# Layer-0 attention loop: keys in two halves instead of three batches, and each engine's work of a step in longer runs

## The chip, the cores and the metric

The kernel runs on one core of a Trainium2 chip, as one launch. The metric is the device time of that core in microseconds. Three runs of the kernel before took 2561.23, 2567.15 and 2571.44 us, the median is 2567.15 us. One more execution was taken with the hardware profiler; all readings below come from it. Its engines are called PE (TensorE matmul), PEld (TensorE weight load), DVE (VectorE), ACT (ScalarE), POOL (GpSimd) and SP (SyncE, here the issuer of most DMAs).

## What is computed

Four residual layers with layer normalisation work on the same 2708 x 2708 adjacency matrix and 2708 x 512 features, all in float32. The change lies in layer 0, a masked attention with 8 heads of 64 dimensions:

```python
keys = jnp.einsum('nj,hjk->hnk', node_matrix, Wks)
queries = jnp.einsum('nj,hjk->hnk', node_matrix, Wqs)
values = jnp.einsum('nj,hjk->hnk', node_matrix, Wvs)
atts = jnp.einsum('hqk,hmk->hqm', queries, keys) / key_dim ** 0.5
atts = atts - 1e+16 * (1.0 - adj)[None, :, :]
atts = jax.nn.softmax(atts, axis=-1)
return jnp.einsum('hqm,hmk,hko->qo', atts, values, Wo)
```

Layers 1 to 3 (two graph convolutions and a graph attention with one score vector) follow; the change does not edit their code.

## The kernel before

First, keys, queries and values are projected (to about 208 us of the profile). Then comes the loop of layer 0 (208 to 1237 us), the output product with `Wo`, and the three other layers.

**Items and steps.** The 2708 nodes are 22 chunks of 128 rows (`NC`; the last, `LAST`, has 20). An item of the loop is one chunk of query rows and one pair of heads: 21 x 4 items and one item for the short last chunk with all heads together, 85 in all. In step i the loop works on four items at once: `new` (item i, its scores), `cur` (item i-1, its softmax weights and their transposition), `late` and `old` (items i-2 and i-3, their value sums).

**Scores (L402, L424).** For one item the 2708 keys are cut into three batches of 1024, 1024 and 660 (`ends`), each into two parts. For each part PE makes one product per head into a PSUM bank (64 x 512 or 64 x 330; float32, so every product shows as two matmul instructions). DVE reads the bank, adds the mask row, writes the scores to SBUF and keeps the maximum: 12 such instructions per item. L439 reduces the maxima.

**Weights (L446).** ACT takes the exponentials in place, one per batch and head: six per item.

**Transposition.** The value sums need the weights with keys on partitions. For 16 of the 22 key chunks (0 to 15, "dealt") DVE transposes 32 x 32 blocks into a tile `d` (L453, four instructions of 128 x 1024 per item), and four DMAs issued by SP (L463, `deal`, 256 KB each) carry the tile from partition to partition into a tile `e`. An item has two deals, one per batch of 8 chunks. The remaining six chunks are transposed by PE (L482, L489, L491, `turn`) into PSUM and copied to SBUF by ACT.

**Value sums (L509).** 22 key chunks x 2 heads, two instructions each, 88 per item, accumulate into one PSUM bank; ACT copies it out (L529) and POOL stores it.

**Order.** PE, DVE and ACT run the loop in the order in which it is written (`tc.manual_schedule`); a planner orders the other queues, SP's and POOL's, by its own costs. On PE a step is: two parts of scores, 8 chunks of value sums of `old`, two parts of scores, 14 chunks of value sums of `late`, two parts of scores, 12 transposes of `cur`. On DVE: four score instructions, the block transposes of the first batch, four score instructions, the block transposes of the second batch, four score instructions, the maxima. So the first deal of `cur` starts in the middle of a step and is used by `late` about one step later, and the second starts near the step's end and is used by `old` in the step after the next.

**Buffers.** PSUM has 8 banks: 2 x 2 for scores (`ps_s`), 3 for PE transposes (`ps_t`), 1 for value sums (`ps_a`). In SBUF there are five score tiles, two tiles `d` and three tiles `e`; a block transpose that reuses a tile `d` waits until the deal that read it has landed. Of the mask for the next chunk, one third is loaded (L169), summed (L187), given its diagonal (L201) and scaled (L207) in each of three of the four steps of a chunk.

Of the kernel before, what the change touches and what calls it, by code (L numbers as in the profile page):

```python
# [10 lines left out]
ALU = mybir.AluOpType  # L11
# [11 lines left out]
def kernel(  # L23
# [65 lines left out]
    def rsqrt(dst, v, q, n, tag):  # L89

        y0 = small.tile([P, n], F32, tag=f"{tag}y0", name=f"{tag}_y0")
        t = small.tile([P, n], F32, tag=f"{tag}t", name=f"{tag}_t")
        nc.scalar.activation(t[:q], v, AF.Ln)  # L93
        nc.scalar.activation(y0[:q], t[:q], AF.Exp, scale=-0.5)
        t2 = small.tile([P, n], F32, tag=f"{tag}t2", name=f"{tag}_t2")
        nc.vector.tensor_tensor(t2[:q], y0[:q], y0[:q], ALU.mult)
        t3 = small.tile([P, n], F32, tag=f"{tag}t3", name=f"{tag}_t3")
        nc.vector.scalar_tensor_tensor(t3[:q], t2[:q], -0.5, v, ALU.mult, ALU.mult)
        nc.vector.scalar_tensor_tensor(dst, t3[:q], 1.5, y0[:q], ALU.add, ALU.mult)
# [18 lines left out]
    ND = ends[2]  # L118
    KD4 = P // 32
    SW = max(min(b * P, N) - a * P for a, b in zip(ends, ends[1:]))  # L120
# [6 lines left out]
    smt = [const.tile([P, HALF0, 2 * NP, NW], F32, tag=f"smt{i}", name=f"smt{i}") for i in range(2)]  # L127
# [10 lines left out]
    with ExitStack() as l0:  # L138
# [70 lines left out]
        with tc.tile_pool(name="kvw", bufs=1) as kvw, tc.tile_pool(name="xTb", bufs=2) as xtp, tc.tile_pool(  # L209
# [64 lines left out]
            for b in order:  # L274
# [15 lines left out]
                for c in chunks_of(b):  # L290
# [3 lines left out]
                    if c < ND:  # L294
# [79 lines left out]
        ps_t = l0.enter_context(tc.tile_pool(name="ps_t", bufs=3, space=PSUM, reuse_waits="tile"))  # L374
        ps_a = l0.enter_context(tc.tile_pool(name="ps_a", bufs=1, space=PSUM, reuse_waits="tile"))
        ps_s = l0.enter_context(tc.tile_pool(name="ps_s", bufs=2, space=PSUM, reuse_waits="tile"))
        sp = l0.enter_context(tc.tile_pool(name="sp", bufs=5, reuse_waits="tile"))
        dp = l0.enter_context(tc.tile_pool(name="dp", bufs=2, reuse_waits="tile"))
        ep = l0.enter_context(tc.tile_pool(name="ep", bufs=3, reuse_waits="tile"))
        ptp = l0.enter_context(tc.tile_pool(name="ptp", bufs=1, reuse_waits="tile"))  # L380

        class Pair:


            def __init__(self, c, p):
                self.c, self.p = c, p
                self.s = []
                self.mx = [
                    small.tile([P, 2 * NW], F32, tag=f"mx{j}", name=f"mx{c}_{p}_{j}") for j in range(2)
                ]  # L390
# [20 lines left out]
            def scores(self, k, part):  # L411
# [3 lines left out]
                n0, w = batch(k)  # L415
                if part == 0:
                    self.s.append(sp.tile([P, 2, SW], F32, tag="s", name=f"s{c}_{p}_{k}"))
                s = self.s[k]
                h0 = part * (w // 2)
                hw = w - w // 2 if part else w // 2  # L420
                pss = [ps_s.tile([P, BLK], F32, tag=f"s{j}", name=f"pss{c}_{p}_{k}_{part}_{j}") for j in range(2)]
                self.products(pss, n0 + h0, hw)
                for j in range(2):
                    nc.vector.tensor_tensor_reduce(  # L424
                        out=s[:, j, h0 : h0 + hw],
                        in0=pss[j][:, :hw],
                        in1=a[:, n0 + h0 : n0 + h0 + hw],
# [4 lines left out]
                        accum_out=self.mx[j][:, 2 * k + part : 2 * k + part + 1],  # L432
                    )

            def maxima(self):
                c, p = self.c, self.p
                self.nm = [small.tile([P, 1], F32, tag=f"nm{j}", name=f"nm{c}_{p}_{j}") for j in range(2)]
                for j in range(2):
                    nc.vector.tensor_reduce(self.nm[j], self.mx[j], AX.X, ALU.max, negate=True)  # L439

            def weights(self, k):

                w = batch(k)[1]
                for j in range(2):
                    s = self.s[k][:, j, :w]
                    nc.scalar.activation(s, s, AF.Exp, bias=self.nm[j], accum_out=self.sums(j, k))  # L446

            def blocks(self, k, j):

                n = ends[k + 1] - ends[k]  # L450
                if k not in self.D:
                    self.D[k] = dp.tile([P, KD4, 2, n, 32], F32, tag="d", name=f"d{self.c}_{self.p}_{k}")
                nc.vector.transpose(  # L453
                    self.D[k][:, :, j].rearrange("p i m x -> p m i x"),
                    self.s[k][:, j, : n * P].rearrange("p (m i x) -> p m i x", i=KD4, x=32),
                )

            def deal(self, k):

                n = ends[k + 1] - ends[k]  # L460
                e = ep.tile([P, KD4, 2, n, 32], F32, tag="e", name=f"e{self.c}_{self.p}_{k}")
# [5 lines left out]
                self.E[ends[k]] = e  # L467

            def turn(self):

                c, p = self.c, self.p
                last = NC - 2
                o, mr = (NC - 1 - ND) * P, rows(NC - 1)[1]

                def part(j, m):
                    return self.s[2][:, j, (m - ND) * P : (m - ND) * P + P]

                for j in range(2):
                    pt = ps_t.tile([P, last - ND, P], F32, tag="t", name=f"pst{c}_{p}_{j}")
                    sb = ptp.tile([P, last - ND, P], F32, tag="pt", name=f"pt{c}_{p}_{j}", bufs=2)  # L480
                    for m in range(ND, last):
                        nc.tensor.transpose(pt[:, m - ND, :], part(j, m), ident)  # L482
                    nc.scalar.copy(sb, pt)  # L483
                    for m in range(ND, last):
                        self.pts[m, j] = sb[:, m - ND, :]
                pt = ps_t.tile([P, 4, P], F32, tag="t", name=f"pst{c}_{p}_2")
                sb = ptp.tile([P, 2, P], F32, tag="pt2", name=f"pt{c}_{p}_2")
                for j in range(2):
                    nc.tensor.transpose(pt[:, j, :], part(j, last), ident)  # L489
# [911 lines left out]
```

## Time and profile before

| | us |
|---|---|
| runs, median (lowest to highest) | 2567.15 (2561.23 to 2571.44) |
| span of the profiled execution, first to last instruction | 2565.8 (its own device time is not listed apart; the median stands 1.35 above the span) |
| stages of the span: projections / loop of layer 0 / the rest | 0 to 208 / 208 to 1237 / 1237 to 2566 |
| busy in 270 to 740, of 470.0: PE, DVE, ACT | 469.2, 456.7, 378.1 |
| the same stretch: granted TensorE clock, DMA share, DMA rate | 1.00, 0.84, 220 GB/s |
| first and last instruction of L439 (two per step): start | 216.5 and 1209.6 |

A group of the profile has the line of the kernel, the engine, what is written and read, the shape and the count, then busy time and the mean of one instruction. The chain is followed back from the last instruction to what released each; in order of time its pieces have start, length, engine, tile and line. In the table of stretches, each engine has its busy time and in brackets its number of instructions, followed by the granted clock, the share of time that the 16 DMA engines were busy, and the rate.

### The profile page before, as it was taken

To read this page: it belongs to the slowest core of one execution; us is meant where nothing else is said; L and a number is where in the kernel's file an instruction comes from. 1 tells how busy PE (TensorE), PEld (TensorE's weight loads), DVE (VectorE), ACT (ScalarE), POOL (GpSimd) and SP (SyncE) were. 2 spreads that over 40 slices of the span, in tenths; PEclk is the share of its full clock that TensorE was granted. 3 is DMA by queue.
4 is the path that set the end of the run, shared out by engine and by line. 5 is a ranking of instruction groups with operands and counts; after the bars stand their busy time and mean duration, and the time that the engine had idled before them with its cause. 6 is when DMAs were issued, how large, how long until landed. Compare 5 with 4: busy or idle time off the path is not lost.

```text
span 2565.8 us, 42805 instructions
## 1 busy us (share of the span) xinstructions
PE 2511.8 (98%) x15551; PEld 1523.6 (59%) x15551; DVE 1958.5 (76%) x4711; ACT 1208.1 (47%) x2410; POOL 315.9 (12%) x322
## 2 busy tenths in 40 slices
PE   9999999999999999999999999899999999999997
PEld 4886766667676767666555445444444466444465
DVE  2669999999999999999474778987876874443544
ACT  2105788787887887887011002565665540000000
POOL 1210000000000000000310000343433430000000
PEclk9999999999999999999899999999999999999999
DMA  5115888888888888888753444444433214644633
GB/s 176 45 58 135 228 217 213 231 212 231 221 208 233 212 213 235 215 215 197 223 174 106 124 118 142 133 155 125 140 109 110 57 30 115 191 139 143 177 99 109
DMA packets 221502, 411.46 MB, mean 160 GB/s; under 512 B 28765, under 2 KB 48911, under 8 KB 221292
## 3 DMA queue, kind: packets, MB, share of 16 engines
q1 hardware_dynamic: 215052, 392.00, 56.0%
q0 software_dynamic: 6240, 16.73, 1.7%
q8 instruction: 123, 2.02, 0.3%
q14 instruction: 87, 0.71, 0.1%
HBM read 213.55 MB, written 16.72 MB: 90 GB/s over the span
## 4 chain that ended last, share of the span: by engine, by line
PE 78%; issue 9%; DVE 7%; DMA 3%; ACT 1%; SPq 1%; POOL 0%; POOLq 0%; DVEq 0%; ACTq 0%
PE pss L402 15%; PE av L509 15%; PE acc L823 12%; PE acc L929 7%; PE m L1233 6%; PE pst L482 3%; PE pf L835 3%; PE po L769 2%; PE psk L253 2%; PE psv L253 2%; PE psq L253 2%; DMA e<-d 2%; PE ph L915 1%; DVE d L453 1%; DVE s L424 1%
## 5 line engine op out<-in xcount | busy, mean ns | idle before, releaser
L424 DVE CUSTOM_DVE_ANT_0 s<-pss,adj 128x512 f32<-128x512 f32 (+1 forms) x1020 | 574.3, 618 | 23.2 <-PE pss L402 21.3
L446 ACT ACTIVATE s<-s,nm 128x1024 f32<-128x1024 f32 (+1 forms) x510 | 527.7, 1037 | 26.6 <-DVE nm L439 25.0
L402 PE MATMUL pss<-KT,qt 64*128 64x512 f32 (+1 forms) x2016 | 460.2, 565 | 4.2 <-DVE mx L424 4.2
L453 DVE STREAM_TRANSPOSE d<-s 128x1024 f32<-128x1024 f32 x340 | 402.4, 1222 | 9.7 <-ACT s L446 4.8
L823 PE MATMUL acc<-pt,x 128*128 128x512 f32 (+1 forms) x880 | 334.7, 539 | 12.0 <-ACT pt L876 9.7
L509 PEld LDWEIGHTS av<-e,V 128*64 128x64 f32 x5376 | 294.6, 137 | 62.7 <-DMA e<-d 41.7
L509 PE MATMUL av<-e,V 128*64 128x128 f32 x5376 | 326.3, 274 | 0.0
L402 PEld LDWEIGHTS pss<-KT,qt 64*128 64x128 f32 x2016 | 191.8, 186 | 140.5 <-issue 67.7
L823 PEld LDWEIGHTS acc<-pt,x 128*128 128x128 f32 x880 | 158.7, 193 | 187.7 <-issue 162.7
L929 PE MATMUL acc<-at,h 128*128 128x512 f32 (+1 forms) x504 | 196.8, 543 | 0.0
L887 POOL TENSOR_TENSOR cs<-cs,pt 128x512 f32<-128x512 f32 (+2 forms) x110 | 157.3, 1430 | 202.9 <-ACT pt L876 199.8
L874 DVE TENSOR_TENSOR pt<-pt,at 128x512 f32<-128x512 f32 (+2 forms) x132 | 107.3, 820 | 74.6 <-ACT pt L873 74.2
L530 POOL DMA_DIRECT2D otd<-ot x84 | 45.2, 538 | 965.4 <-ACT ot L529 953.0
L1263 ACT ACTIVATE z<-pz,rdeg 128x512 f32<-128x512 f32 (+1 forms) x22 | 15.1, 688 | 311.1 <-PE pz L835 311.1
L93 ACT ACTIVATE ln_t<-lnve 128x1 f32<-128x1 f32 x88 | 17.7, 201 | 301.5 <-DVE lnve L107 301.3
L929 PEld LDWEIGHTS acc<-at,h 128*128 128x128 f32 x504 | 90.2, 190 | 101.4 <-issue 99.0
L483 ACT COPY pt<-pst 128x512 f32<-128x512 f32 x170 | 91.4, 589 | 120.4 <-PE pst L482 120.3
L509 PEld LDWEIGHTS av<-pt,V 128*64 128x64 f32 x1680 | 90.0, 136 | 64.6 <-ACT adj L187 46.2
L876 ACT ACTIVATE pt<-pt 128x512 f32<-128x512 f32 (+2 forms) x132 | 76.1, 578 | 108.8 <-DVE pt L875 108.7
L940 DVE SCALAR_TENSOR_TENSOR cs<-at,rdeg,cs 128x512 f32<-128x512 f32 (+2 forms) x126 | 86.2, 684 | 40.8 <-DMA at<-in_adjT_dram 39.7
L509 PE MATMUL av<-pt,V 128*64 128x128 f32 x1680 | 110.3, 278 | 1.4 <-ACT ot L529 1.4
L482 PEld LDWEIGHTS pst<-ident,s 128*128 128x128 f32 x680 | 73.5, 141 | 38.8 <-issue 38.3
(352 smaller groups left out, 3627.6 us busy)
## 6 DMA issues: line engine op xcount, KB each, us to landing
e<-d SPq DMA_DIRECT2D x680, 256.0 KB
at<-in_adjT_dram SPq DMA_DIRECT2D x210, 256.0 KB
a<-in_adj_dram SPq DMA_DIRECT2D x38, 677.0 KB
adj<-in_adj_dram SPq DMA_DIRECT2D x42, 512.0 KB
at_a<-in_adjT_dram SPq DMA_DIRECT2D x40, 256.0 KB
at_c<-in_adjT_dram SPq DMA_DIRECT2D x40, 256.0 KB
at_f<-in_adjT_dram SPq DMA_DIRECT2D x40, 256.0 KB
adj<-in_adj_dram SPq DMA_DIRECT2D x21, 330.0 KB
```

Of the source, the lines that this page charges most:

```text
L253: nc.tensor.matmul(ps[:, p, :], ws[i][:, k, p * P : (p + 1) * P], xs[i][:, k, :], start=(k == 0), stop=(k == FC - 1),)
L402: nc.tensor.matmul(pss[j][:, :w], qt[h, self.p, :], KT[h, self.p, n0 : n0 + w], start=True, stop=True)
L424: nc.vector.tensor_tensor_reduce(out=s[:, j, h0 : h0 + hw], in0=pss[j][:, :hw], in1=a[:, n0 + h0 : n0 + h0 + hw], scale=1.0, scalar=LOW, o ...
L446: nc.scalar.activation(s, s, AF.Exp, bias=self.nm[j], accum_out=self.sums(j, k))
L453: nc.vector.transpose(self.D[k][:, :, j].rearrange("p i m x -> p m i x"), self.s[k][:, j, : n * P].rearrange("p (m i x) -> p m i x", i=KD4 ...
L482: nc.tensor.transpose(pt[:, m - ND, :], part(j, m), ident)
L509: nc.tensor.matmul(self.av[j * KD : (j + 1) * KD, out], V[:, m, h * KD : (h + 1) * KD], weights[j], start=(self.done == 0), stop=(self.don ...
L823: nc.tensor.matmul(acc[k][:, :w], last[0][g : g + mr, :] if m == NC - 1 else values[:mr, k * P : (k + 1) * P], moving[g : g + mr, :w], sta ...
L874: nc.vector.tensor_tensor(pt[:mr, :w], pt[:mr, :w], at[:mr, :w], ALU.subtract)
L887: nc.gpsimd.tensor_tensor(sums[:mr, :w], sums[:mr, :w], pt[:mr, :w], ALU.add)
L929: nc.tensor.matmul(acc[hc][:, :w], lastH[g : g + mr, :] if m == NC - 1 else H[m][:mr, hc * P : (hc + 1) * P], at[g : g + mr, :w], start=(m ...
L1233: nc.tensor.matmul(acc[k][:, : moving.shape[1]], combined[which, m][:, k * P : (k + 1) * P], moving, start=(m == 0), stop=(stop and m == N ...
```

## The change

The keys are cut into two halves, 1408 and 1300 (`bounds`), each into three parts of 469, 469, 470 and 433, 433, 434 keys. In each half the first 8 chunks are dealt (0 to 7 and 11 to 18); PE transposes the other six (8, 9, 10, 19, 20, 21). The exponentials are four per item, the block transposes two per item (each for both heads, 2048 columns), the maxima one instruction. Scores and PE transposes share 7 PSUM banks in rotation; the bank of the value sums stays. Score tiles are two per half; tiles `d` and `e` stay two and three.

The written order of a step is now: on PE all scores of `new`, all value sums of `late` (the PE-transposed chunks first, then the two deals), all transposes of `cur`; on DVE all 12 score instructions, the maxima, the two block transposes of `cur`, each followed by its deal; on ACT the exponentials of `cur`'s second half, the work on the next mask, the exponentials of `new`'s first half, the copy of the value sums, the copies of the transposes. `old` is gone, and the loop has one step less at its end. In `rsqrt`, scratch tiles that are wider than one column get one buffer instead of four.

```diff
     NW = 3
     ends = [0, 8, 16, NC]
-    ND = ends[2]
+    HALVES = 2
+    PARTS = 3
+    DEALT = 8
+    bounds = [0, NC // 2, NC]
+    def dealt(c):
+        return any(a <= c < a + DEALT for a in bounds[:-1])
+    turned = [c for c in range(NC) if not dealt(c)]
...
-                    if c < ND:
+                    if dealt(c):
...
-        ps_t = l0.enter_context(tc.tile_pool(name="ps_t", bufs=3, space=PSUM, reuse_waits="tile"))
         ps_a = l0.enter_context(tc.tile_pool(name="ps_a", bufs=1, space=PSUM, reuse_waits="tile"))
-        ps_s = l0.enter_context(tc.tile_pool(name="ps_s", bufs=2, space=PSUM, reuse_waits="tile"))
-        sp = l0.enter_context(tc.tile_pool(name="sp", bufs=5, reuse_waits="tile"))
+        ps_s = l0.enter_context(tc.tile_pool(name="ps_s", bufs=7, space=PSUM, reuse_waits="tile"))
+        sp = l0.enter_context(tc.tile_pool(name="sp", bufs=2, reuse_waits="tile"))
         dp = l0.enter_context(tc.tile_pool(name="dp", bufs=2, reuse_waits="tile"))
         ep = l0.enter_context(tc.tile_pool(name="ep", bufs=3, reuse_waits="tile"))
...
+        ready = turned + [c for c in range(NC) if dealt(c)]
...
-                h0 = part * (w // 2)
-                hw = w - w // 2 if part else w // 2
+                h0, h1 = (w * i // PARTS for i in (part, part + 1))
...
-            def blocks(self, k, j):
+            def blocks(self, k):
+                self.D[k] = dp.tile([P, KD4, 2, DEALT, 32], F32, tag="d", name=f"d{self.c}_{self.p}_{k}")
                 nc.vector.transpose(
-                    self.D[k][:, :, j].rearrange("p i m x -> p m i x"),
-                    self.s[k][:, j, : n * P].rearrange("p (m i x) -> p m i x", i=KD4, x=32),
+                    self.D[k].rearrange("p i j m x -> p j m i x"),
+                    self.s[k][:, :, : DEALT * P].rearrange("p j (m i x) -> p j m i x", i=KD4, x=32),
                 )
...
-            def values(self, m0, m1):
+            def values(self):
...
-                for m in range(m0, m1):
+                for m in ready:
...
-            for i in range(len(items) + 3):
+            for i in range(len(items) + 2):
                 if cur is not None:
-                    cur.weights(0)
+                    cur.weights(1)
                 if i < len(items):
...
-                    new.scores(0, 0)
-                    new.scores(0, 1)
-                if old is not None:
-                    old.values(ends[1], ND)
-                if prep:
-                    row_sums(c + 1, p - 1)
-                if cur is not None:
-                    cur.weights(1)
-                    cur.blocks(0, 0)
-                    cur.blocks(0, 1)
-                    cur.deal(0)
...
-                    new.scores(1, 0)
-                    new.scores(1, 1)
-                if cur is not None:
-                    cur.weights(2)
-                if late is not None:
-                    late.values(ND, NC)
-                    late.values(0, ends[1])
-                if cur is not None:
-                    cur.blocks(1, 0)
-                    cur.blocks(1, 1)
-                    cur.deal(1)
...
+                    for part in range(PARTS):
+                        new.scores(0, part)
+                    if prep:
+                        row_sums(c + 1, p - 1)
+                    new.scores(1, 0)
+                    if prep:
+                        loops(c + 1, p - 1)
+                        mask(c + 1, p - 1)
+                    for part in range(1, PARTS):
+                        new.scores(1, part)
                     new.maxima()
+                    new.weights(0)
...
+                if late is not None:
+                    late.values()
                 if cur is not None:
+                    for k in range(HALVES):
+                        cur.blocks(k)
+                        cur.deal(k)
                     cur.turn()
...
-                old, late, cur = late, cur, new
+                late, cur = cur, new
```

## The prediction

> **What bounds the kernel now.** I read the chain first. On the page it is mostly PE:
>
> ```profile
> PE 78%; issue 9%; DVE 7%; DMA 3%; ACT 1%; SPq 1%; POOL 0%; POOLq 0%; DVEq 0%; ACTq 0%
> ```
>
> The same chain in order of time, inside the loop, is PE alone. One step:
>
> ```profile
> 310.93 1.92 PE pss L402 x8
> 312.85 1.90 PE av L509 x32
> 314.74 1.92 PE pss L402 x8
> 316.66 3.21 PE av L509 x56
> 319.87 1.31 PE pss L402 x8
> 321.18 1.02 PE pst L482 x8
> 322.20 0.22 PE pst L489 x2
> 322.42 0.22 PE pst L491 x2
> ```
>
> The pieces add to 11.72 us: PE never waits here. Over the loop the 84 intervals between the maxima (L439, 216.5 to 1209.6 us) average 11.82 us; the 0.1 more is steps in which mask loads get in the way. Next the timeline of DVE, to see how close the second engine is:
>
> ```profile
> 706.55 0.69 DVE L424 CUSTOM_DVE_ANT_0 s<-pss,adj 128x512 f32<-128x512 f32 x1
> ...
> 710.88 0.50 DVE L424 CUSTOM_DVE_ANT_0 s<-pss,adj 128x330 f32<-128x330 f32 x1
> ...
> 711.30 0.50 DVE L424 CUSTOM_DVE_ANT_0 s<-pss,adj 128x330 f32<-128x330 f32 x1
> ...
> 714.59 2.37 DVE L453 STREAM_TRANSPOSE d<-s 128x1024 f32<-128x1024 f32 x2
> ```
>
> Starts are 0.61 us apart at 512 columns (from 706.55 to 707.16) and 0.42 at 330. A step has 8 x 0.61 + 4 x 0.42 + 2 x 2.33 for transposes + 0.37 for maxima and hand-over = 11.6 us of 11.72. DVE is 0.1 us from being the bound. Third, DMA, over one step whose block transposes end at 705.24 and 710.14:
>
> ```profile
> 705.24:707.24 2.00, 2.00 (x42) 2.00 (x40) 2.00 (x8) 2.00 (x5) 0.00 (x0) 1.00 0.39 59
> 707.24:712.24 5.00, 5.00 (x46) 3.54 (x44) 4.87 (x17) 4.14 (x10) 0.00 (x0) 1.00 0.90 210
> 712.24:717.24 5.00, 5.00 (x53) 2.91 (x51) 5.00 (x11) 4.34 (x10) 0.54 (x1) 1.00 0.80 210
> ```
>
> A deal is slow to start (59 GB/s for 2 us) and then runs at 210 GB/s with the DMA engines 80 to 90% busy: 256 KB (262,144 bytes) in 1.25 us. The trace's completion records give the landings: deal one all landed 7.28 us after its block transposes ended, deal two 7.83 us after its own, at 717.97. Nobody waits: `late` reads the first at 718.0 (landed 712.5), `old` reads the second at 724.65. What a deal does with something ahead of it in the queue shows near the loop's end:
>
> ```profile
> 1160.57 0.60 SPq L463
> 1161.22 1.10 SPq L463
> 1162.66 5.49 DMA e<-d
> 1168.37 2.37 DVE d L453 x2
> ```
>
> Its transposes had ended at 1158.06; it landed at 1168.15, 10.1 us later, and DVE stood waiting for tile `d`.
>
> **The change part by part.** Lengths are from the profiled execution, and the sum is made on its span of 2565.8 us.
>
> *PE gains.* 24 value-sum instructions more take 3.21 - 1.90 = 1.31 us: 54.6 ns each, so a run costs 0.15 us to enter (1.90 - 32 x 0.0546). A score run of 8 costs 1.92 us at 512 columns and 1.31 at 330: 3.35 ns a column, 0.20 to enter. Going from three score runs to one and from two value runs to one saves 2 x 0.20 + 0.15 = 0.55 us: 11.72 becomes 11.17 us. Twelve banks through a rotation of seven cost nothing: the hiding work is DVE's 0.55 us per bank against PE's 0.40; if PE had no lead left, its run would stretch to DVE's pace, up to 1.6 us, still beside DVE's work.
>
> *DVE gains little.* The columns are the same. From 0.61 and 0.42, (0.61 - 0.42)/182 = 1.04 ns a column; 469 columns cost 0.565 us, 433 cost 0.527; six of each 6.55. One reduction instead of two, with hand-over, 0.25; two transposes of 2048 columns 2.3 each (two of 1024 took 2.37). Sum 11.4 us, call it V. Without new waits the step would be the larger of 11.17 and 11.4.
>
> *ACT.* Exponentials of 1024 take 1.14 us and of 660 take 0.83, so 1408 take 1.47 and 1300 take 1.38: 5.7 us instead of 6.2. With mask work (1.25 + 1.14) and copies (2.2) it has 10.3 us of work in the fullest steps. New order: the copies that free PSUM banks queue behind `new`'s first exponentials, which wait for the maxima. At 11.4 us a step this leaves about 1 us of slack; beyond that scores would wait for banks.
>
> *The deals lose their lead: the cost.* Both deals now start at the end of DVE's step, 2.3 us apart instead of 5 to 7, and `late` reads both in the very next step. Call L the time from the end of the second block transposes to the landing of the second deal. It is not seen directly. From below: a deal by itself, 7.6 us. From above: 10.1 us as at 1158, plus what mask loads in front add (deals behind three mask loads landed after 8.64 and 9.72 us instead of 7.28 and 7.83), about 12. Between: eight DMAs back to back take 2 + 8 x 1.25 = 12.0 us from the end of the first block transposes by the rate; by the landings in the step above 12.7 us (705.24 to 717.97, no pause in between). Less the 2.3 us, L is 9.7 to 10.4. I take 10.2, nearest to the landings.
>
> From that landing the path runs on PE: the last 32 value instructions 1.75, twelve transposes 1.46, entries 0.3, then the next scores until DVE can begin, 1.1 (PE started at 722.73 and DVE at 723.89 with 512 columns): 4.6 us. PE works in order, so the next scores cannot pass the waiting value sums. Then comes DVE's whole step V to the end of its second block transposes. A deal issued at the end of step n holds back the scores of step n+2, so two steps take 2T = L + 4.6 + V = 10.2 + 4.6 + 11.4 = 26.2, T = 13.1 us. This is above both engines' own times, so it sets the pace. A second wait lies just under it: the second block transposes reuse tile `d`, which the deal of the step before still reads, T >= L + 2.3 = 12.5.
>
> *SP.* It still issues eight deal DMAs a step, and the third and fourth of a deal were held 1.0 to 1.5 us each at issue; now eight stand in one row, and the mask loads (1.6 MB per four steps) queue among them. Before they cost the mean 0.1 us a step; I keep that: T = 13.2 us.
>
> *The end of the loop.* Before, the load of `wo` was issued at 1221.5, 12 us after the last maxima, right behind the last deal. Now both deals of the last item follow two block transposes that wait for tile `d`: between -3 (one step less) and +9 us; I take +4. Everything with one answer: dealing chunks 11 to 18 instead of 8 to 15 changes addresses of as many POOL copies, the scratch buffers of `rsqrt` are used one step at a time, the dropped `old` adds no work: 0.
>
> Sum: (13.2 - 11.82) x 84 = +116, +4 at the end: 2565.8 + 120 + 1.35 (median over span) = 2687 us, +4.7%.
>
> **Two rules weighed.** The Trainium skill, "DMA: Bandwidth & Descriptors", section on the anatomy of one DMA (it describes the gpsimd path), gives about 2.0 us plus bytes at 436 GB/s. As an estimate by that page, both deals would be through 2.0 + 4.8 = 6.8 us after the first block transposes, L = 4.5, and the step would be DVE's 11.4. The rows above moved the same bytes at half that rate, so the measurement decides.
> "TensorE: Matmul & The Clock Gate", section on HAM oscillation, warns that idle gaps over about 3.4 us halve PE's clock. The rows show clock 1.00 in 270 to 740 us, where PE idled 0.8 of 470 us, so no row tests it inside the loop. If each pair of steps tripped one such window, the page would add, as an estimate, 42 x 1.7 = 71 us.
>
> **The rivals.**
> - *No new wait.* If a second deal needed L <= 2 x 11.4 - 4.6 - 11.4 = 6.8 us and tile `d` came free in time, T = 11.4: 2567 - 0.42 x 84 = 2532 us. For it: PE and DVE both have less to do. Against: even a deal alone took 7.3 to 7.8.
> - *The gain and the wait cancel.* L = 7.6, as if the first deal did not delay the second: T = 11.8, 2567 us. Against: 80 to 90% busy DMA engines with two deals half as close.
> - *Deals stream faster back to back.* At 1.1 us per DMA instead of 1.25 (single pairs of landings in that step are 0.74 to 1.13 us apart), the start of 2.7 us that the 12.7 contain gives L = 2.7 + 8.8 - 2.3 = 9.2: T = 12.6, 2633 us. Against: the mean over eight was 1.25 to 1.28.
> - *Mask loads land in front of the deals.* If the planner puts 1.6 MB there every fourth step, each delays a deal by up to 3 us, half of which a step in the pair regains: T = 13.8, 2738 us.
> - *The runs do not form*: banks come late because ACT's copies do, and PE's entries stay. Then 11.7 us a step plus the wait: 13.2, the forecast's own time.
>
> **How the numbers follow.** Forecast (T 12.7 to 13.7: 2640 to 2730) 0.50; faster streaming (2580 to 2640) 0.18; masks in front (over 2730) 0.12; cancelled (within 0.5%, about what a measurement of this kernel can tell from no change: 2554 to 2580) 0.08; no new wait (below 2554) 0.12. The range 2575 to 2750 leaves out the last two and the far tail of the third: about 2 in 10.
>
> **What would show it.** Score instructions 0.53 to 0.57 us apart, runs of 24 score and 88 value instructions: the change does what it says. Right: PE weight loads of L509 wait for `e` DMAs near the middle of their run, DVE idles 1 to 3 us before the first L424 of a step, long and short steps may alternate, the loop takes about 13 us a step, the clock stays at 1.00. Wrong: landings within 7 us of the second block transposes, or a chain that stays on DVE with 11.4 us steps; then the DMA rate that I carried over was a rate of demand, not a limit.

## The result, and the profile after

The kernel after takes 2750.03 us (median of four runs, 2738.09 to 2756.89), beside 2567.13 us for the kernel before: ratio 1.0713, 95% interval 1.0679 to 1.0747. The forecast was 2687 us with a range up to 2750: the direction and the mechanism were those forecast, the loss is about half as large again (183 us instead of 120).

The profiled execution is the fastest of the four, 2738.09 us with a span of 2736.3 us. The chain that ended last is of no use here: 52% of it is "issue", because followed back it strays to POOL's stores of the value sums (L527) and loses the loop. The engines' own timelines have to be read. PE over three steps of the loop (start, length, engine, line, tiles, shape, count; in brackets idle time and what ended it):

```profile
643.48 5.06 PE L417 MATMUL pss<-KT,qt 64*128 64x469 f32 x24
648.47 1.31 PE L508 MATMUL av<-pt,V 128*64 128x128 f32 x20
649.61 0.39 PE L508 MATMUL av<-lastT,V 128*64 128x128 f32 x4
650.30 1.97 PE L508 MATMUL av<-e,V 128*64 128x128 f32 x32 [0.30 <-DMA e<-d]
654.81 3.42 PE L508 MATMUL av<-e,V 128*64 128x128 f32 x32 [2.55 <-DMA e<-d]
658.16 1.53 PE L489 MATMUL pst<-ident,s 128*128 128x128 f32 x12
659.62 5.05 PE L417 MATMUL pss<-KT,qt 64*128 64x469 f32 x24
...
682.05 1.97 PE L508 MATMUL av<-e,V 128*64 128x128 f32 x32 [2.22 <-DMA e<-d]
```

The runs are there: 24 score instructions, 88 value instructions, 12 transposes. In the middle of the value sums PE stands still for the second deal, 2.55 and 2.22 us. And the 32 sums after that wait took 3.42 us at 654.81, but 1.97 at 682.05: the same work, once at half the clock. DVE over the same steps:

```profile
651.48 2.31 DVE L463 STREAM_TRANSPOSE d<-s 128x2048 f32<-128x2048 f32 x1
654.80 2.31 DVE L463 STREAM_TRANSPOSE d<-s 128x2048 f32<-128x2048 f32 x1 [1.02 <-DMA e<-d]
660.71 0.65 DVE L439 CUSTOM_DVE_ANT_0 s<-pss,adj 128x469 f32<-128x469 f32 x1 [3.59 <-PE pss L417]
...
667.61 4.51 DVE L463 STREAM_TRANSPOSE d<-s 128x2048 f32<-128x2048 f32 x2
672.11 0.65 DVE L439 CUSTOM_DVE_ANT_0 s<-pss,adj 128x469 f32<-128x469 f32 x1
```

DVE's step from 644.57 to 660.71 lasts 16.1 us, with a wait for tile `d` and then a long one for scores; the next, 660.71 to 672.11, lasts 11.4 us with no wait at all. Long and short steps alternate. Now the stretches: the whole loop from first to last maxima, in the profile before and in this one, then the 12 us in which two deals move (block transposes ended at 642.38 and 644.57; columns as explained above):

```profile
217.00:1210.00 993.00, 987.58 (x10382) 687.65 (x10381) 962.50 (x2554) 797.61 (x1619) 44.65 (x83) 1.00 0.83 217
...
217.00:1357.00 1140.00, 1004.94 (x10328) 742.07 (x10327) 957.71 (x2304) 754.93 (x1279) 44.66 (x83) 0.97 0.76 187
644.38:649.38 5.00, 5.00 (x38) 2.96 (x36) 5.00 (x18) 3.06 (x6) 0.00 (x0) 1.00 0.92 209
649.38:654.38 5.00, 2.58 (x44) 2.13 (x40) 4.33 (x10) 2.91 (x4) 0.00 (x0) 1.00 0.91 248
654.38:656.38 2.00, 1.57 (x16) 1.60 (x18) 1.58 (x1) 0.10 (x2) 0.00 (x0) 0.51 0.75 160
```

PE is busy in 1005 of 1140 us; before it was busy in 988 of 993. DVE's busy time is as before (958, before 962 us). The DMA engines are over 90% busy while two deals move, and idle more over the loop as a whole (0.76, 0.83 before). The granted clock falls to 0.51 right after PE's wait. The waits in the loop (who waits, for whom: us in total, times, longest):

```profile
DVE s L439 <- PE pss L417: 130.7, 54, 4.9
PE av L508 <- DMA e<-d: 128.0, 83, 4.0
...
DVE d L463 <- DMA e<-d: 39.3, 30, 2.8
```

PE waits 128 us for deals; DVE waits 131 us for the scores that stand behind PE's wait, the same time seen one engine on.

Where the 170.5 us of span came from: the 84 steps between maxima average 13.57 us instead of 11.82, +146.4; the first maxima are 0.7 us later; the rest of the program after the last maxima takes 1379.6 instead of 1356.2 us, +23.4. Of these, 15.3 us lie between the last maxima and the first product with `Wo` (43.0 instead of 27.7), 4.9 in that product's stage, 4.8 in layer 2, -1.6 elsewhere.

### The profile page after: what moved, and what is told of

The parts are those of the page before. It is cut to its first block, busy times and chain, and to the rows that moved or that the text cites. A ratio compares the mean times of both kernels' runs of the same rounds, so it can differ in the third digit from the quotient of the medians.

```text
span 2736.3 us, 42432 instructions
## 1 busy us (share of the span) xinstructions
PE 2542.3 (93%) x15551; PEld 1587.4 (58%) x15551; DVE 1959.5 (72%) x4456; ACT 1166.5 (43%) x2070; POOL 315.1 (12%) x322
## 4 chain that ended last, share of the span: by engine, by line
issue 52%; PE 39%; DVE 4%; POOL 2%; DMA 1%; ACT 1%; SPq 0%; POOLq 0%; ACTq 0%; DVEq 0%
PE acc L803 12%; PE acc L909 7%; PE m L1213 4%; PE po L749 2%; PE pf L815 2%; PE psk L261 2%; POOL otd L527 2%; PE ph L895 1%; PE psv L261 1%; PE psq L261 1%; PE p L940 1%; PE psv L357 1%; PE acc_t L803 1%; PE psq L309 1%; PE pz L815 1%
## 5 line engine op out<-in xcount | busy, mean ns | idle before, releaser
L439 DVE CUSTOM_DVE_ANT_0 s<-pss,adj 128x469 f32<-128x469 f32 (+2 forms) x1020 | 567.2, 623 | 131.5 <-PE pss L417 131.3
L458 ACT ACTIVATE s<-s,nm 128x1408 f32<-128x1408 f32 (+1 forms) x340 | 480.9, 1415 | 226.8 <-DVE nm L452 226.8
L508 PE MATMUL av<-e,V 128*64 128x128 f32 x5376 | 353.4, 290 | 133.7 <-DMA e<-d 133.4
L417 PE MATMUL pss<-KT,qt 64*128 64x469 f32 (+2 forms) x2016 | 430.5, 554 | 4.3 <-ACT pt L495 2.7
L463 DVE STREAM_TRANSPOSE d<-s 128x2048 f32<-128x2048 f32 x170 | 387.3, 2300 | 51.4 <-DMA e<-d 46.1
L508 PEld LDWEIGHTS av<-e,V 128*64 128x64 f32 x5376 | 325.4, 147 | 153.4 <-issue 151.2
L417 PEld LDWEIGHTS pss<-KT,qt 64*128 64x128 f32 x2016 | 217.2, 186 | 177.8 <-issue 141.4
L527 POOL DMA_DIRECT2D otd<-ot x84 | 45.2, 538 | 1128.4 <-ACT ot L526 1100.1
L489 PE MATMUL pst<-ident,s 128*128 128x128 f32 x1020 | 133.4, 281 | 1.0 <-ACT s L458 1.0
L489 PEld LDWEIGHTS pst<-ident,s 128*128 128x128 f32 x1020 | 107.4, 136 | 19.2 <-issue 16.3
```

Of the source, the lines that this page charges most:

```text
L417: nc.tensor.matmul(pss[j][:, :w], qt[h, self.p, :], KT[h, self.p, n0 : n0 + w], start=True, stop=True)
L439: nc.vector.tensor_tensor_reduce(out=s[:, j, h0:h1], in0=pss[j][:, : h1 - h0], in1=a[:, n0 + h0 : n0 + h1], scale=1.0, scalar=LOW, op0=ALU ...
L458: nc.scalar.activation(s, s, AF.Exp, bias=self.nm[:, j : j + 1], accum_out=self.sums(j, k))
L463: nc.vector.transpose(self.D[k].rearrange("p i j m x -> p j m i x"), self.s[k][:, :, : DEALT * P].rearrange("p j (m i x) -> p j m i x", i= ...
L489: nc.tensor.transpose(pt[:q, t, j, :], self.s[f][:, j, o : o + q], ident)
L508: nc.tensor.matmul(self.av[j * KD : (j + 1) * KD, out], V[:, m, h * KD : (h + 1) * KD], weights[j], start=(self.done == 0), stop=(self.don ...
```

## The experiments

The theory: the second deal lands too late, and because PE works in order it holds back the scores of the step after, once every two steps; the clock then adds to it. The rivals: tile `d` sets the pace; the mask loads in the queue do; longer runs cost something in themselves (banks, ACT). Ratios below are against the kernel before on the same chip, with 95% intervals; "step" is the mean distance of maxima in the loop.

**1. Take the transfers away.** Everything stays, but no deal is issued and the sums read one constant tile: the moving of the weights is left out.

```diff
+        still = ep.tile([P, KD4, 2, DEALT, 32], F32, tag="still", name="still", bufs=1)
+        nc.gpsimd.memset(still, 0.01)
...
-                e = ep.tile([P, KD4, 2, DEALT, 32], F32, tag="e", name=f"e{self.c}_{self.p}_{k}")
-                for g in range(KD4):
-                    nc.sync.dma_start(
...
-                self.E[bounds[k]] = e
+                self.E[bounds[k]] = still
```

> The changed kernel without the deals: the eight DMAs per item are left out and the value sums of the dealt chunks read one constant tile (this leaves out moving the weights, so the output is not the reference's). All instructions of PE, DVE and ACT stay. Deal theory: with nothing to wait for, the step is DVE's own 11.4 us, the clock stays at 1.00 in the loop, and the whole takes about 2750 - 2.17 x 84 - 10 = 2558 us (2535 to 2575). Rival, long runs cost the time: 2650 or more.

Measured: 2542.87 us in one run, beside 2569.91; step 11.43 us. PE's timeline of one step of it:

```profile
641.79 5.06 PE L420 MATMUL pss<-KT,qt 64*128 64x469 f32 x24
648.13 3.67 PE L505 MATMUL av<-still,V 128*64 128x128 f32 x64
```

So the longer runs cost nothing: they would gain 0.4 us a step, down to DVE's own 11.4, as worked out. All of the loss, and the gain that never came, hang on the deals. Which wait it is, this run does not tell.

**2. A third tile `d`** (paid for with one tile `e`), against the rival that DVE's wait for tile `d` sets the pace.

```diff
-        dp = l0.enter_context(tc.tile_pool(name="dp", bufs=2, reuse_waits="tile"))
-        ep = l0.enter_context(tc.tile_pool(name="ep", bufs=3, reuse_waits="tile"))
+        dp = l0.enter_context(tc.tile_pool(name="dp", bufs=3, reuse_waits="tile"))
+        ep = l0.enter_context(tc.tile_pool(name="ep", bufs=2, reuse_waits="tile"))
```

> The changed kernel with three tiles d instead of two (and two tiles e instead of three, to find the space): the second block transposes no longer wait for the deal of the step before. Deal theory (PE's in-order wait is the pace): the 39 us that DVE waits there lie beside that wait and nearly nothing is gained, 2725 to 2755 us. Rival, tile d sets the pace: the step falls by the wait, 2650 to 2700 us.

Measured: 2749.83 us, 1.0688 (1.0670 to 1.0706), the time of the kernel after. Of its waits:

```profile
DVE s L439 <- PE pss L417: 198.5, 47, 7.7
...
PE av L508 <- DMA e<-d: 134.4, 81, 4.2
```

DVE no longer waits for tile `d` at all, and its wait for scores is longer, 199 us instead of 131. (The profile is of the slowest of five executions, 2763.32 us, with 116 us of the loop at half clock; that of the kernel after is of its fastest, with 78.5.) The tile `e` that was given up cost little: SP waited for PE's value sums ahead of deals for 20 us in all, in the kernel after for 3. Tile `d` was not the pace.

**3. Something for PE to do in the wait that is on its path anyway.** The transposes of `cur` are put between the sums of the first deal and those of the second.

```diff
                 if late is not None:
-                    late.values()
+                    late.values(first)
                 if cur is not None:
...
                     cur.turn()
+                if late is not None:
+                    late.values(second)
```

> The changed kernel with one edit in PE's order: the twelve transposes of cur stand between the value sums of the first deal and those of the second, instead of behind them. Deal theory: the path from the landing to the next scores loses the transposes' 1.46 us (4.6 becomes 3.2), two steps take 10.1 + 3.2 + 11.4 = 24.7, 12.35 us a step, just under which tile d lies with 12.4; the idle stretch on PE gets shorter, so fewer half-clock windows: 2750 - 1.2 x 84 = about 2650 us (2630 to 2680). Rival, the pace is set by tile d alone: no change, 2735 or more.

Measured: 2660.97 us, 1.0349 (1.0317 to 1.0381); step 12.68. On PE:

```profile
646.97 1.53 PE L490 MATMUL pst<-ident,s 128*128 128x128 f32 x12
649.30 1.97 PE L509 MATMUL av<-e,V 128*64 128x128 f32 x32 [0.80 <-DMA e<-d]
651.19 5.06 PE L418 MATMUL pss<-KT,qt 64*128 64x469 f32 x24
```

Scores now follow the late sums at once. The path is shorter by the 1.46 us of the transposes every two steps, 61 us over the loop; the time at half clock also fell from 78.5 to 10.2 us. At 1.7 us of lost work per window of 3.4 that would be another 34 us, 95 in all; the ratio moved by 0.036, or 93 us (the loops of the two profiled executions differ by 74 us). To see the clock's part by itself took the next run.

**4. Work that is good for nothing.** The kernel after with twelve identity transposes, whose result nobody reads, between the two deals' sums: 1.5 us of added PE work a step, only to keep PE busy.

```diff
-                    late.values()
+                    late.values(first)
+                    if late.c < LAST:
+                        idle = bank([P, 4, P], f"idle{i}")
+                        for k in range(12):
+                            nc.tensor.transpose(idle[:, k % 4, :], ident, ident)
+                    late.values(second)
```

> The changed kernel with added work: twelve PE transposes of the identity into an unused bank (1.3 us of PE time a step, read by nobody) between the value sums of the first deal and those of the second, where PE idles in the long steps. Clock theory: the filler keeps the idle stretch too short to halve the clock, the 78 us at half clock in the loop mostly go, and with them up to 39 us; in the short steps the filler delays PE within the slack that the alternation leaves: about 2715 us (2700 to 2735), granted clock 0.985 or more. Rival, the half-clock windows cost nothing because they fall into waits: 2745 to 2800 us.

Measured: 2717.59 us, 1.0563 (1.0544 to 1.0582): more work, and 0.015 faster, 38 us. Of the 78.5 us at half clock in the loop 10.2 are left. A step of it on PE:

```profile
651.97 1.53 PE L646 MATMUL idle<-ident 128*128 128x128 f32 x12
653.61 1.97 PE L509 MATMUL av<-e,V 128*64 128x128 f32 x32
```

The second sums run at full speed, 1.97 us instead of 3.42. No other work or wait leaves the path: in steps 10 to 79, where no half-clock window stands, two steps together take 26.8 us here and 26.4 in the kernel after, so the filler by itself costs some 16 us over the loop, and the gain is the clock's. How large it is depends on the executions compared. The two profiled ones, the fastest of the kernel after and the slowest of this run, differ by 17 us of span and 12 us in the loop; with the 16 us that the filler costs, the clock's share of the loop is about 28 us there, and more between the medians.

**5. The first deal earlier**, in the middle of DVE's step.

```diff
                         row_sums(c + 1, p - 1)
+                if cur is not None:
+                    cur.blocks(0)
+                    cur.deal(0)
+                if i < len(items):
                     new.scores(1, 0)
...
-                    for k in range(HALVES):
-                        cur.blocks(k)
-                        cur.deal(k)
+                    cur.blocks(1)
+                    cur.deal(1)
```

> The changed kernel with one edit: the block transposes of the first half, and the deal behind them, stand after the first six score instructions of DVE's step instead of at its end. PE's and ACT's orders are untouched. Deal theory: the second deal no longer queues behind the first, so it lands about 7.8 us after its block transposes instead of 10.1, two steps take 7.8 + 4.6 + 11.4 = 23.8, 11.9 us a step instead of 13.57, and the idle windows that halve PE's clock mostly go: 2750 - 1.67 x 84 = about 2610 us (2580 to 2640). Rival, the long runs themselves cost the time (PSUM banks, PE's order): nothing changes, 2720 us or more. Rival, the reuse of tile d sets the pace: it would also fall, to about the same 2600, so this run does not separate the two deal paths.

Measured: 2659.59 us, 1.0338 (1.0311 to 1.0364); step 12.71. A miss by 50 us. In steps 10 to 79 two of four steps took 11.6 to 11.8 us (one of them 12.2), as expected, a third 12.1 to 13.7, and every fourth 13.3 to 18.6: there a query load and two mask loads stood ahead of the second deal on SP's queue, and it landed 9.0 to 11.2 us after its transposes; most other second deals landed after 7.1 to 8.3. A new wait stood beside it, PE for banks that ACT had yet to copy out:

```profile
PEld pss L417 <- ACT pt L495: 71.1, 108, 1.6
```

**6. The second deal used one step later**, by an item `old`, as the kernel before does; this takes a second bank for value sums, and leaves six for scores.

```diff
-        ps_a = l0.enter_context(tc.tile_pool(name="ps_a", bufs=1, space=PSUM, reuse_waits="tile"))
-        ps_s = l0.enter_context(tc.tile_pool(name="ps_s", bufs=7, space=PSUM, reuse_waits="tile"))
+        ps_a = l0.enter_context(tc.tile_pool(name="ps_a", bufs=2, space=PSUM, reuse_waits="tile"))
+        ps_s = l0.enter_context(tc.tile_pool(name="ps_s", bufs=6, space=PSUM, reuse_waits="tile"))
...
+                if old is not None:
+                    old.values(second)
                 if late is not None:
-                    late.values()
+                    late.values(first)
...
-                late, cur = cur, new
+                old, late, cur = late, cur, new
```

> The changed kernel with the value sums of the second deal read one step later, as the kernel before did (old), in the same run of 88 value instructions on PE; PSUM banks 6 for scores and 2 for value sums. DVE's order is untouched, so both deals still start together and tile d is still reused after one step. Deal theory with PE's in-order wait as the pace: that wait is gone; the next bound is tile d, at least 10.2 + 2.3 = 12.5 us a step: 2750 - 1.07 x 84 = about 2660 us (2620 to 2690), with DVE waiting for e DMAs before its second block transposes. Rival, tile d had set the pace all along: nothing gained, 2730 or more.

Measured: 2625.55 us, 1.0210 (1.0183 to 1.0236); step 12.35. PE waits for the second deal no more; what is left among the waits is the one that the prediction put "just under it", and one for banks:

```profile
PEld pss L418 <- DVE mx L440: 114.9, 370, 2.1
...
DVE d L464 <- DMA e<-d: 41.8, 51, 2.2
```

This undoes the main wait by the one thing that the change dropped, a step of lead, and gives back 70% of the loss (0.050 of 0.071), although scores lose a bank by it. It is the direct evidence for the theory; the half-clock time in the loop goes with the wait, from 78.5 to 10.2 us, and is part of these 70%.

**7. Both moved:** 5 and 6 together. On the kernel after:

```diff
+                if cur is not None:
+                    cur.blocks(0)
+                    cur.deal(0)
+                if i < len(items):
                     new.scores(1, 0)
...
+                if old is not None:
+                    old.values(second)
                 if late is not None:
-                    late.values()
+                    late.values(first)
...
-                    for k in range(HALVES):
-                        cur.blocks(k)
-                        cur.deal(k)
+                    cur.blocks(1)
+                    cur.deal(1)
```

> Both edits together: the first deal starts mid step and the second deal is read a step later. Deal theory: no wait is left above DVE's work, 11.4 to 11.6 us a step against 11.82 before: 2535 to 2575 us, at or a little below the kernel before. Rival, DMA throughput itself is the floor (eight deal DMAs of 1.25 us plus mask loads): 11.8 to 12.2 us a step, 2575 to 2620 us.

Measured: 2613.16 us, 1.0166 (1.0145 to 1.0187); step 12.32. A miss: no deal is waited for on PE, yet the step is 0.9 us above DVE's own. ACT's timeline shows why:

```profile
657.51 1.47 ACT L459 ACTIVATE s<-s,nm 128x1408 f32<-128x1408 f32 x1 [4.90 <-DVE nm L453]
...
660.58 1.07 ACT L496 COPY pt<-pst 128x512 f32<-128x512 f32 x2
```

ACT waits 4.90 us for the maxima, and the copies that free PE's banks stand behind the exponentials that waited; PE then waits for banks (71 us in the loop), DVE for PE (62 us). This is the slack of "about 1 us" of the prediction's ACT part, used up (here with six banks instead of seven).

**8. Copies first.** As 7, with `new`'s first exponentials moved behind the copies, to the start of the next step.

```diff
                 if cur is not None:
+                    cur.weights(0)
                     cur.weights(1)
...
                     new.maxima()
-                    new.weights(0)
```

> Both deal edits, and one more in ACT's order: the exponentials of the new item's first half stand behind the copies out of PSUM (at the start of the next step, ahead of the second half's) instead of in front of them. Theory from the run with both deal edits: there the wait left is ACT standing idle for the maxima with the copies queued behind the exponentials, so the banks of the PE transposes come free late and the scores wait, 12.3 us a step. With the copies first the step falls to DVE's 11.4 to 11.6: 2613 - 0.8 x 84 = about 2545 us (2535 to 2565), below the kernel before. Rival, DMA throughput is the floor: the step stays at 11.8 to 12.3, 2570 to 2613 us.

Measured: 2594.12 us, 1.0083 (1.0068 to 1.0098); step 11.97. ACT's wait is gone, worth 0.008; the rest of the miss shows in PE's score run, 5.62 us where seven banks gave 5.05:

```profile
645.62 5.62 PE L418 MATMUL pss<-KT,qt 64*128 64x469 f32 x24
```

With six banks the twelve products run at DVE's pace near their end.

**9. One bank for both open sums**, so that scores have seven again.

```diff
+        both = ps_a.tile([P, 2, P], F32, tag="av", name="avs")
...
-                    self.av = ps_a.tile([P, P], F32, tag="av", name=f"av{c}_{p}")
+                    self.av = both[:, p % 2, :]
```

> As the run with the copies first, but the two value sums that are open at a time share one PSUM bank (256 of its 512 columns), so scores and transposes have seven banks again instead of six. Theory from the run before: there PE's score run took 5.62 us instead of 5.05, held up for banks by DVE, and 0.57 us of the 11.97 us step is that. Expected 11.5 us a step, 2594 - 0.45 x 84 = about 2556 us (2545 to 2570), 0.5% below the kernel before. Rival, the score run is paced by DVE's own order (block transposes in the middle) whatever the banks: no change, 2585 to 2600.

Measured: 2713.15 us, 1.0548 (1.0523 to 1.0574); step 13.40. A miss. The score run is 5.06 us as expected, but sums in one tile wait for ACT to read the other half of that tile:

```profile
661.55 1.40 PE L511 MATMUL avs<-pt,V 128*64 128x128 f32 x20 [2.47 <-ACT ot L531]
```

A new wait of 2.5 us in place of one of 0.6 us, and with it 58 us at half clock.

**10. Sums between scores.** As 8, with `old`'s sums between the first eight and the last four score products, so that six banks are enough for each run.

```diff
+                if old is not None:
+                    old.values(second)
+                if i < len(items):
                     for part in range(1, PARTS):
...
-                if old is not None:
-                    old.values(second)
```

> As the run with the copies first (six banks for scores and transposes, two for value sums), and on PE the value sums of the second deal stand between the first eight and the last four score products, at the time when DVE makes block transposes and frees no bank. PE enters a run twice more (0.35 us), 11.5 us of its own time a step. Theory: the 0.57 us in which the score run waits for banks goes, the step is 11.5 to 11.6 us instead of 11.97: 2594 - 0.4 x 84 = about 2560 us (2550 to 2572), at or a little below the kernel before. Rival, DMA or ACT holds the step at 11.97: 2590 to 2600.

Measured: 2602.45 us, 1.0143 (1.0113 to 1.0172); step 12.11. A miss, and slower than run 8. In steps 10 to 79 three of four steps took 11.3 to 11.7 us, except five of 12.1 to 13.3; the fourth took 12.2 to 14.5, once 17.4. In it a query load and two mask loads stand in one row on SP's queue (at 677.87 us, for one) with a deal behind them, and the third mask load behind that. DVE then waits for tile `d`, up to 4.7 us at a time:

```profile
DVE d L464 <- DMA e<-d: 30.9, 14, 4.7
```

**11. The loads where they are written.** As 10, and SP's queue too runs in the written order, which places the loads one third per step.

```diff
-            engines={mybir.EngineType.PE, mybir.EngineType.DVE, mybir.EngineType.Activation}
+            engines={mybir.EngineType.PE, mybir.EngineType.DVE, mybir.EngineType.Activation, mybir.EngineType.SP}
```

> As the run with the value sums between the score products, and SP's queue too runs the loop in the written order: the three mask loads and the query load of a chunk then stand one in each step instead of three or four in a row. Theory: in the run before, three of four steps took 11.3 to 11.5 us and every fourth 12.5 to 14, when a row of loads delayed a deal until the block transposes waited for tile d. Spread out they fit beside the deals: 11.5 to 11.7 us in every step, 2602 - 0.5 x 84 = about 2560 us (2545 to 2575). Rival, the DMA engines lack the time altogether (10 us of deals and 1.5 us of loads a step): the mean stays at 12.0 or above, 2590 to 2610.

Measured: 2556.40 us, 0.9938 (0.9921 to 0.9954): below the kernel before by 0.6%, little but outside the interval. Step 11.54 us. In the loop PE is busy in 968 of 973 us, and the granted clock is 1.00:

```profile
217.00:1190.00 973.00, 967.68 (x10364) 687.69 (x10363) 959.34 (x2307) 743.58 (x1280) 44.76 (x83) 1.00 0.89 221
```

The same deals and loads as in runs 7 to 10 fit into 11.54 us a step, so the rival named there, that DMA throughput is the floor, falls. Run 8 with this edit alone was not tried; whether run 10's edit is needed is not shown.

**12. The control**: the edit of SP's order alone, on the kernel before.

```diff
-            engines={mybir.EngineType.PE, mybir.EngineType.DVE, mybir.EngineType.Activation}
+            engines={mybir.EngineType.PE, mybir.EngineType.DVE, mybir.EngineType.Activation, mybir.EngineType.SP}
```

> The kernel before with that one edit, SP's queue in the written order. Theory: its steps are bound by PE at 11.72 us, and only the 0.1 us that mask loads add on the mean can go: 2571 - 8 = 2560 to 2571 us, not to be told from no change. Rival, the spread loads delay its deals, too: above 2585.

Measured: 2564.94 us, 0.9975 (0.9965 to 0.9985); step 11.77. So of the 0.62% in run 11, 0.25% would have come to the kernel before as well, and what is left, about 0.4%, is what the regrouping is worth together with the edits of runs 7, 8 and 10, once both deals have their lead back.

## Why the prediction was right in direction and short in size

- *The runs and the engines' own work: right.* Score starts on DVE are 0.565 to 0.57 us apart at 469 columns and 0.53 at 433; DVE's undisturbed step is 11.4 us (V); without deals the loop runs at 11.43.
- *The late second deal: right.* The time from the second block transposes to the landing, L, was forecast at 10.2. In the 42 steps between 10 and 79 whose two block transposes ran back to back it averaged 10.25 us (9.6 to 11.3); from 644.57 to 654.68 it was 10.1, and 9.8 in the step after 672.12. The DMA engines were 91 to 92% busy for most of that time, at 209 to 248 GB/s, so the carried-over rate of 210 held. The estimate from the Trainium skill, "DMA: Bandwidth & Descriptors", section on the anatomy of one DMA, L = 4.5, does not hold for these landings (the page's fit is for the gpsimd path, the deals are issued by SP): they took more than twice as long.
- *The path from landing to the next scores: right at full clock.* From 681.92 to 686.50 it took 4.58 us, forecast 4.6.
- *The pair of steps: right.* In steps 10 to 79 of the loop, the 19 pairs (a long step and the short one behind it) that no half-clock window touches average 26.4 us. The forecast was 26.2, and 26.4 with the 0.1 us a step for mask loads. Rival by rival: "no new wait", "cancelled" and "faster streaming" fall with L. "Mask loads in front" named nearly the measured time (2738 us), but not the mechanism: of the 42 second deals above, the 20 with a mask or query load among them or up to 4 us ahead landed after 10.4 us on average, the 22 without after 10.2, where the rival needed up to 3 us. Loads in front of a deal show as a cost in runs 5 and 10.
- *The clock: this is the step that failed.* The prediction said "the clock stays at 1.00" and left the estimate for half-clock windows, 42 x 1.7 = 71 us, out of the sum, since "no row tests it inside the loop". The runs show the term: 78.5 us of the loop at half clock, 23 windows of 3.4 us, where before had one. So about one pair in two tripped a window, not each. The 16 pairs of steps 10 to 79 that a window touches average 27.9 us, 1.5 more than the others. The untouched pairs, carried over the loop, give (13.2 - 11.82) x 84 = 116 us, as forecast; measured are 146, and the 30 us left over are about 1.3 us for each window (39 us, an estimate, if each cost the full half of its length). Run 4 says the same from the other side, some 28 us between the two profiles. The reason given for leaving the term out was not good either: the stretch just ahead of the one that was read shows a window inside the loop of the kernel before, at 224.9 us, where PE stood idle for 2.3 us of 53:

```profile
217.00:270.00 53.00, 50.73 (x441) 32.80 (x440) 50.25 (x132) 42.67 (x85) 1.63 (x3) 0.97 0.74 194
```

- *The loop's end: mis-sized.* Forecast +4 with bounds of -3 and +9; it was +15.3. The last items' sums wait for deals three times more (2.90, 1.68 and 0.53 us after one of 0.82), the load of `wo` is issued 22.0 us after the last maxima instead of 12, behind 24 deal DMAs that stand in one row on SP, and 30.7 us at half clock lie between 1367 and 1406 us where before had 17.1. I had counted only the wait for tile `d`.
- *The rest of the program: forecast at 0, came out at +8.1 us.* The profile after has one short half-clock window more than the profile before in the product with `Wo`, and two more in layer 2; at 1.7 us each, an estimate, they would make 5 of the 8 us. No run separates them from other causes; this stays open.

In all, in terms of span: 2685.8 forecast, +30 in the loop beyond the forecast and +1 ahead of it, +11 at the loop's end, +8 later: 2736. The median lies another 12 us above the profiled execution. The two longest executions, 18 to 19 us above it, had a granted clock of 0.970 instead of 0.974; by clock and span, an estimate, that is some 23 us more at half clock, or 12 us of lost work. The rest of that difference is open.

## What to carry to other kernels

Grouping work into long runs on an in-order engine saves entries of a fraction of a microsecond, and moves the producers together as well: reckon for each transfer the lead that is left between its start and its first reader, at the rate that a busy moment of the trace shows, and put behind it the path back to the next producer. A stop of some two microseconds on PE cost more than its length here, because the clock followed it down in about every second pair of steps; if such a stop can't be removed, try to put work into it that is on the path anyway (run 3), or even work that is not (run 4). And when one wait is removed, name the next: here lead for both deals, the order of ACT's copies, the banks and the place of loads in SP's queue each showed up as a wait on the way, and with all of them set right the regrouping paid 0.4%.

## What I had not expected of the hardware

- *How little idle time halves the clock.* In the profile of the kernel after, half-clock stretches begin on a fixed grid of 3.413 us and last one step of it, some of them two or more. All 21 grid windows in the loop in which PE was idle, by the profile, for 2.07 to 2.90 us in total were followed by half clock; of the full-clock windows with 2.01 us or less only one was (1.92 us, in the loop's last step). The Trainium skill, "TensorE: Matmul & The Clock Gate", section on HAM oscillation, speaks of idle gaps over about 3.4 us; here about 2.0 us inside one window was enough. The edge is neither sharp nor the same in every program: with a third tile `d` a window of 1.93 us triggered and one of 1.96 did not; with one bank for sums ten of 1.98 and one of 1.58 triggered, and one of 2.01 did not; in the kernel before the window ahead of the one at 224.9 us had 0.9 us. Why, no run shows.
- *More work, less time.* 1.5 us a step of matmuls that nobody reads made the program 1.4% faster (1.0563 against 1.0713).
- *Two halves of one PSUM tile are one thing to wait for.* Sums that write the one half waited 2.5 us for ACT's read of the other (run 9). Whether the chip needs this wait or only the program's own bookkeeping of tiles was not tried.
